# Graph-and-convolution layer: pieces for graph and gates, three streams stepped in turn, PSUM split by stage, vector work paced by size

## The chip, the core and the metric

The kernel runs on one core of a Trainium2 chip. The metric is the device time of one execution in microseconds (us); the time of a version is the median of its runs. The core's engines work side by side, each through its own list of instructions in order: PE multiplies matrices (PEld loads its weights), DVE does vector work, ACT evaluates functions, POOL does vector work too, SP issues the DMAs. PE writes its results to PSUM, which has eight banks of 128 x 512 float32; the other engines read them from there. Everything here is float32.

## The reference

For each of 32 batches x is 512 x 256 (nodes by features) and adj 512 x 512. Cut to what is computed:

```python
h = jnp.maximum(_layernorm(x, axis=-1), 0.0)
x = x + ref(h, adj, ...)

def ref(x, mask, ...):                                  # x is the normalised h
    xc = jnp.transpose(x, (0, 2, 1))
    h = jax.nn.relu(_bn(_conv1d(xc, conv1_w, 0), ...))   # 1 tap
    h = _bn(_conv1d(h, conv2_w, 8), ...)                 # 17 taps
    x_conv = jnp.transpose(jax.nn.relu(h + xc), (0, 2, 1))
    s = x @ w_se.T + b_se                                # 3 columns
    sq = jnp.sum(s * s, axis=-1)
    dist = sq[:, :, None] + sq[:, None, :] - 2.0 * jnp.einsum('bnd,bmd->bnm', s, s)
    A = jnp.exp(-dist) * mask
    msg = jax.nn.relu(x @ w_msg.T + b_msg)
    x_nmp = jnp.einsum('bnm,bmd->bnd', A, msg)
    x_in = jnp.concatenate([x_conv, x_nmp], axis=-1)
    gi, gh = x_in @ w_ih.T + b_ih, x @ w_hh.T + b_hh     # three gates each
    r, z = sigmoid(gi_r + gh_r), sigmoid(gi_z + gh_z)
    nn_ = jnp.tanh(gi_n + r * gh_n)
    return (1.0 - z) * nn_ + z * x
```

## The kernel before

The batches go in 8 groups of 4. Three stages work on three successive groups at once.

**Stage one** takes the batches of group g+1 one by one. `norm` gives DVE statistics (L189, L190), a POOL power (L146) and a scaling (L197) of the loaded `x_sb`; `norm_t` transposes it (PE L216, ACT L217) to `hT`, which also goes to DRAM as `hd`. `begin` ends with the load of batch b+2 (L97) and puts its `norm` on a list. `graph` then makes four `messages` (PE product to a PSUM bank, DVE bias L489/L490, ACT relu L493), the five small DVE steps of `factors` (L497 to L503), their transposes (L508, L512), `kernel_exp` (four small products L522, four ACT exponentials L526), four `masked` steps (PE transposes an `m_sb` block of adj, L533; DVE multiplies, L535) and two `gather` products, whose result goes to DRAM as `nd`. `rows` does the one-tap convolution into `h1` (ACT L226).

**Convolution.** The 17 taps are done for a group as 25 products with fewer multiplications. The operand of each is made by DVE from `h1`: five long ones `x1` (1,415 columns) and 25 short ones (471 columns), L237 and L240. At most four wait ahead (`AHEAD`), and the last rows of the next group may overwrite `h1` only once the 21st operand is made (`freed`, "rows wanted"). A product is two halves of four matmuls into `ps_c`; its weights `w` are read again from DRAM for each product (L339, two ahead). `summed` reads the products (ACT L368, L382; DVE L377, L379, L385, L386) and puts the additions that follow (DVE L355, L362, ACT L358) and, at the end of the group, eight evacuations (ACT L409, into `xconv`) on the list `SUMS`.

**Stage three** (`gates`) takes the batches of group g-1. `xconv` gets `hT` added (DVE L628) and a relu (ACT L629). For each half o of the features, four gate sums follow: hidden part of n, then r, z and the given part of n, each as one uninterrupted `matmul_sum` of 2 to 6 matmuls of 512 columns. Then DVE (L653, L667), ACT (L651, L661, L668) and three POOL steps (L674 to L676) make `o_sb`. `finish` transposes it back (PE L550), adds the residual (DVE L554) and stores it. It is called by `finish_waiting`, in the middle of the next `graph` after `kernel_exp`, or else after the first product of the next `gates`.

What sets the order on each engine is the order in which this program is written out; no scheduler moves anything (`manual_schedule`). `others` strings stage one and stage three together: the whole graph of one batch, then the whole gates of another. The loop at the end steps either `others` or one half of a convolution product, by a balance of their lengths; a "gap" in the graph calls for one half product. `pace` is called with the length of each PE step and puts vector work in between: it takes in turn from `SUMS`, the operands, the norms and, at first, the preparation of the convolution's weights, while its credit is positive. It has

```python
credit = min(credit + pe * 0.8, 4.0)
...
credit -= 0.9          # for each piece of work, whatever its length
```

Before the first group `first` does stage one of group 0 without a convolution, and what is left of the preparation is done behind it in one row. After the last group the gates of its four batches run alone, each step taking one piece from `SUMS`. Of the eight PSUM banks `ps_c` has two, `ps_acc` four (messages, rows, kernel, gather and gates share them) and `ps_tr` two (all transposes).

## Time and profile before

| | us |
|---|---|
| median of 3 runs | 2787.89 (2783.47 to 2789.23) |
| profiled execution | 2796.92 |
| its span, first to last instruction | 2795.1 |
| PE busy in it | 2402.3 (86%) |
| DVE busy | 1163.0 (42%) |
| ACT busy | 639.8 (23%) |
| POOL busy | 301.5 (11%) |
| first convolution product | 172.3 |
| mean granted TensorE clock | 0.923 of full speed |

The profiled execution is 9.0 us above the median. A row of waits says which engine at which line waited for what, and the total; a row of the timeline begins with the time from the start of the span and the length. "<-" names what ended an idle time. PE's busy time contains whatever a reduced clock adds to its instructions, so a busy PE is not PE at full speed.

### The profile page before, as it was taken

What the parts mean: (1) busy time and instruction counts of PE and PEld (TensorE: products, weight loads), DVE (VectorE), ACT (ScalarE), POOL (GpSimd) and SP (SyncE); (2) the same over time, 40 slices, a digit from 0 to 9 for tenths busy, and PEclk for the clock granted to TensorE, in tenths of its full rate; (3) what the DMA queues carried; (4) which work ended last, traced back from release to release, by engine and by line L of the source; (5) the groups of instructions that cost most, each with busy time, mean ns of one, the idle gap of its engine ahead of it and who ended that gap; (6) DMA issues with size and microseconds to landing.
All of it is one profiled execution on the core that took longest, in us unless ns stands there. A gap on an engine that the chain in (4) does not pass through costs nothing. (4 is left out here: it accounts for less than half of the span.)

```text
span 2795.1 us, 21712 instructions
## 1 busy us (share of the span) xinstructions
PE 2402.3 (86%) x8224; PEld 1516.8 (54%) x8224; DVE 1163.0 (42%) x1989; ACT 639.8 (23%) x930; POOL 301.5 (11%) x239
## 2 busy tenths in 40 slices
PE   5757878898889888889988889888899899999888
PEld 3446655555555555555555655555555555565543
DVE  5565543434544234353343532435333443454311
ACT  3321222122322123212132122321123122211211
POOL 1000001100111100111010111010111010112122
PEclk8879988999999999999999999999999999999999
DMA  5443332322322323322223322223222232223210
GB/s 195 145 180 128 114 129 84 113 83 94 105 94 89 107 72 106 109 90 87 83 98 106 103 90 87 91 98 113 80 98 81 89 112 87 83 91 102 72 61 27
DMA packets 132280, 277.88 MB, mean 99 GB/s; under 512 B 11984, under 2 KB 61520, under 8 KB 131536
## 3 DMA queue, kind: packets, MB, share of 16 engines
q1 hardware_dynamic: 132176, 276.50, 29.6%
q8 instruction: 65, 1.06, 0.2%
q14 instruction: 39, 0.32, 0.0%
HBM read 213.01 MB, written 63.44 MB: 99 GB/s over the span
## 5 line engine op out<-in xcount | busy, mean ns | idle before, releaser
L90 PE MATMUL ps_c<-x,w 128*128 128x228 f32 x3200 | 753.4, 387 | 125.1 <-issue 60.3
L90 PEld LDWEIGHTS ps_c<-x,w 128*128 128x128 f32 x3200 | 657.7, 209 | 237.3 <-issue 142.4
L90 PE MATMUL ps_acc<-xconv,wih 128*128 128x512 f32 x768 | 364.7, 597 | 13.1 <-ACT xconv L629 13.1
L90 PE MATMUL ps_acc<-hTb,whh 128*128 128x512 f32 x768 | 360.9, 602 | 5.3 <-DMA hTb<-hd 5.3
L90 PE MATMUL ps_acc<-xnb,wih 128*128 128x512 f32 x768 | 361.6, 593 | 0.0
L653 DVE SCALAR_TENSOR_TENSOR r<-ps_acc,vec,r 128x512 f32<-128x512 f32 x64 | 48.0, 751 | 615.4 <-ACT r L651 615.4
L674 POOL TENSOR_TENSOR gate_t<-hTb,r 128x512 f32<-128x512 f32 x64 | 88.2, 1378 | 1969.0 <-issue 1393.9
L90 PEld LDWEIGHTS ps_acc<-xnb,wih 128*128 128x128 f32 x768 | 146.1, 190 | 186.0 <-issue 186.0
L90 PEld LDWEIGHTS ps_acc<-xconv,wih 128*128 128x128 f32 x768 | 146.8, 191 | 178.4 <-issue 163.3
L90 PE MATMUL ps_acc<-at,msg 128*128 128x512 f32 x512 | 238.2, 620 | 5.0 <-DVE at L535 3.0
L90 PEld LDWEIGHTS ps_acc<-hTb,whh 128*128 128x128 f32 x768 | 147.9, 194 | 152.9 <-issue 146.2
L667 DVE TENSOR_TENSOR r<-ps_acc,r 128x512 f32<-128x512 f32 x64 | 44.2, 691 | 382.1 <-PE ps_acc L90 381.8
L533 PE MATMUL ps_tr<-ident,m_sb 128*128 128x128 f32 x512 | 92.9, 330 | 123.2 <-DVE at L535 62.1
L90 PEld LDWEIGHTS ps_acc<-at,msg 128*128 128x128 f32 x512 | 104.9, 206 | 122.2 <-issue 116.9
L240 DVE SCALAR_TENSOR_TENSOR x<-x,x 128x471 f32<-128x471 f32 (+1 forms) x184 | 160.2, 870 | 4.3
L237 DVE TENSOR_TENSOR x<-x 128x471 f32<-128x471 f32 x200 | 157.3, 803 | 1.4
L533 PEld LDWEIGHTS ps_tr<-ident,m_sb 128*128 128x128 f32 x512 | 71.0, 168 | 143.2 <-DVE at L535 90.3
L543 ACT ACTIVATE xnmp<-ps_acc 128x512 f32<-128x512 f32 x64 | 38.2, 597 | 464.3 <-PE ps_acc L90 464.3
L90 PE MATMUL ps_acc<-wmsg,hT 128*128 128x259 f32 x512 | 128.3, 394 | 10.4 <-ACT hT L217 10.4
L237 DVE TENSOR_TENSOR x<-h 128x1415 f32<-128x1415 f32 x40 | 83.2, 2098 | 94.0 <-ACT h L226 94.0
L661 ACT ACTIVATE z<-ps_acc,brz 128x512 f32<-128x512 f32 x64 | 44.0, 687 | 331.1 <-PE ps_acc L90 331.1
L90 PE MATMUL ps_acc<-hT,w 128*128 128x512 f32 x256 | 118.8, 612 | 0.1
(94 smaller groups left out, 1944.0 us busy)
## 6 DMA issues: line engine op xcount, KB each, us to landing
w<-wd SPq DMA_DIRECT2D x200, 512.0 KB, 3.6
m_sb<-in_adj_dram SPq DMA_DIRECT2D x128, 256.0 KB, 3.0
x_sb<-in_x_dram SPq DMA_DIRECT2D x32, 512.0 KB, 4.9
hd<-hT SPq DMA_DIRECT2D x32, 512.0 KB, 3.0
nd<-xnmp SPq DMA_DIRECT2D x64, 256.0 KB, 2.0
hTb<-hd SPq DMA_DIRECT2D x32, 512.0 KB, 4.4
xnb<-nd SPq DMA_DIRECT2D x64, 256.0 KB, 3.8
y<-in_x_dram SPq DMA_DIRECT2D x64, 256.0 KB, 4.1
```

What stands on the lines that cost most here:

```text
L90: nc.tensor.matmul(ps, lhsT, rhs, start=(i == 0), stop=(i == len(pairs) - 1))
L237: nc.vector.tensor_tensor(dst, get(a), get(b), op=ALU.subtract)
L240: nc.vector.scalar_tensor_tensor(dst, a, -2.0, b, op0=ALU.mult, op1=ALU.add)
L533: nc.tensor.transpose(ps[:, c, :], m[:, c * P : (c + 1) * P], ident)
L543: nc.scalar.activation(xnmp, ps, AF.Copy)
L653: nc.vector.scalar_tensor_tensor(r, ps_h, vec[:, _COL["b_hh"] + 2 * ND + o : _COL["b_hh"] + 2 * ND + o + 1], r, op0=ALU.add, op1=ALU.mult,)
L661: nc.scalar.activation(z, ps_z, AF.Sigmoid, bias=brz[:, ND + o : ND + o + 1])
L667: nc.vector.tensor_tensor(r, ps_n, r, op=ALU.add)
L674: nc.gpsimd.tensor_tensor(t, hT[:, o, :], r, op=ALU.subtract)
```

## The change

The arithmetic and the number of instructions on each engine stay as they are, except that two additions in the preparation of the weights become one that multiplies and adds. The pieces, their order and the buffers change:

- PSUM: `ps_acc` has two banks, for the gates alone. Two new banks `ps_g` take messages, rows, gather and two of the four products of `kernel_exp`; the other two of these go to `ps_tr`.
- `gather` is in two pieces, `factors` is called before the step of the fourth message ends, and the graph has no gaps.
- `gates` is written in pieces of two matmuls, split by source (hidden, xconv, xnb), in the order r, hidden n, z, given n. The addition and relu of `xconv` come after the first hidden product, and `finish_waiting` right behind them; the graph no longer calls it. POOL works in place in `o_sb`. Both `xnb` are loaded at the end of the gates before (two buffers instead of three), behind the loads of the residual on SP.
- The rows of all four batches come at the end of stage one.
- Stage one, stage three and the convolution are three streams; the loop steps the one with the least progress.
- `pace` takes a rate and charges each piece by its columns; the credit is capped at 1. ACT's copies and evacuations cost nothing but the constant. It is used behind the last group too, and the preparation is interleaved with stage one of group 0.

```diff
-    acc = ctx.enter_context(tc.tile_pool(name="acc", bufs=4, space=PSUM))
+    acc = ctx.enter_context(tc.tile_pool(name="acc", bufs=2, space=PSUM))
+    gps = ctx.enter_context(tc.tile_pool(name="gps", bufs=2, space=PSUM))
...
-            HT[b] = front.tile([P, ND, N], F32, name="hT", bufs=3)
+            HT[b] = front.tile([P, ND, N], F32, name="hT", bufs=4)
...
-        pss = [acc.tile([P, N], F32, name="ps_acc") for c in range(NT)]
+        pss = [pool.tile([P, N], F32, name=name) for pool, name in 2 * [(gps, "ps_g"), (tr, "ps_tr")]]
...
         for c in range(NT):
             messages(b, msg, c)
+            if c == NT - 1:
+                factors()
             yield 0.93
-        factors()
-        yield gap()
-        yield gap()
         factors_t()
         yield 0.67
-        yield gap()
         kernel_exp(at)
         yield 1.2
-        yield from finish_waiting()
-        yield gap()
         for n in range(NT):
             masked(b, at, n)
             yield 0.55
-        yield gap()
         for d in range(ND):
-            gather(b, msg, at, d)
-            yield 3.46
-        yield from between
+            yield from gather(b, msg, at, d)
...
+        def products(ps, o, g, first, last):
+            parts = [(whh, 0, hT[:, 0, :], hT[:, 1, :])]
+            parts += [(wih, 0, *x_in[:2]), (wih, ND, *x_in[2:])] if x_in else [None, None]
+            for k in range(first, last):
...
+                yield 1.73
         for o in range(ND):
+            yield from products(ps_r, o, 0, 0, 1)
             if o == 0:
+                while b not in evacuated:
+                    SUMS.pop(0)[0]()
+                xconv = XC.pop(b)[:, :, :N]
+                nc.vector.tensor_tensor(xconv, xconv, hT, op=ALU.add)
+                nc.scalar.activation(xconv, xconv, AF.Relu)
                 yield from finish_waiting()
+            yield from products(ps_r, o, 0, 1, 3)
...
+            yield from products(ps_h, o, 2, 0, 1)
...
+            yield from products(ps_z, o, 1, 0, 3)
...
+            yield from products(ps_n, o, 2, 1, 3)
...
-    def pace(pe):
-        credit = min(credit + pe * 0.8, 4.0)
+    def pace(pe, rate):
+        credit = min(credit + pe * rate, 1.0)
...
-            credit -= 0.9
+            credit -= 0.06 + 0.0011 * size
...
+    def stage_one(g):
+        new = range(g * G, (g + 1) * G)
+        for b in new:
+            yield from begin(b)
+            yield from graph(b)
+        yield "rows wanted"
+        for b in new:
+            yield from rows(b)
...
+            streams["one"] = [stage_one(g + 1), 77.0 * 0.86, 0.0]
+            streams["three"] = [stage_three(g - 1), 130.0, 6.0]
+        streams["conv"] = [conv, 82.5 * 0.96, 0.0]
+        rate = 0.4 if g > 0 else 0.7
...
+        while streams:
+            step(min(streams, key=lambda k: streams[k][2] / streams[k][1]))
+    for got in stage_three(NG - 1):
+        pace(got, 1.0)
```

Three places show what this does to the order. The first is PE's list around the masks of one batch in the middle of a group. The names are those of the stages above: `ps_c` is half a convolution product, `hTb,whh`, `xconv,wih` and `xnb,wih` are the three sources of the gates. Before:

```order
L522 MATMUL ps_acc<-right,left 128x512 x4
L550 MATMUL ps_tr<-ident,o_sb 128x128 x8
L90 MATMUL ps_c<-x_2359,w 128x228 x4
L533 MATMUL ps_tr<-ident,m_sb 128x128 x16
L90 MATMUL ps_c<-x_2359,w 128x228 x4
L90 MATMUL ps_acc<-at,msg 128x512 x8
L90 MATMUL ps_acc<-hTb,whh 128x512 x4
```

And now, from the third product of `kernel_exp` on:

```order
L525 MATMUL ps_g<-right,left 128x512
L525 MATMUL ps_tr<-right,left 128x512
L92 MATMUL ps_c<-x_2627,w 128x228 x4
L635 MATMUL ps_acc<-xnb,wih 128x512 x2
L536 MATMUL ps_tr<-ident,m_sb 128x128 x4
L635 MATMUL ps_acc<-hTb,whh 128x512 x2
L92 MATMUL ps_c<-x_2625,w 128x228 x4
L536 MATMUL ps_tr<-ident,m_sb 128x128 x8
L635 MATMUL ps_acc<-hTb,whh 128x512 x2
L536 MATMUL ps_tr<-ident,m_sb 128x128 x4
L92 MATMUL ps_c<-x_2625,w 128x228 x4
```

The sixteen mask transposes of a batch, which stood in a row, are now in groups of four and eight with gate products and half products between, and the finish (L550) is no longer there.

The second is the end of a group's stage one on PE (`ps_acc<-hT` and `ps_g<-hT` are the one-tap convolution). Before:

```order
L533 MATMUL ps_tr<-ident,m_sb 128x128 x16
L90 MATMUL ps_c<-x_2966,w 128x228 x4
L90 MATMUL ps_acc<-at,msg 128x512 x8
L90 MATMUL ps_acc<-hT,w_81 128x512 x12
L90 MATMUL ps_acc<-hTb,whh 128x512 x4
L90 MATMUL ps_acc<-xconv,wih 128x512 x2
L90 MATMUL ps_acc<-xnb,wih 128x512 x2
```

And now, where `x_3163` is the last product of a group and `x_3439` the first of the next:

```order
L635 MATMUL ps_acc<-xnb,wih 128x512 x2
L92 MATMUL ps_c<-x_3163,w 128x228 x4
L92 MATMUL ps_g<-hT,w_84 128x512 x10
L217 MATMUL ps_tr<-ident,x_sb 128x128 x4
L92 MATMUL ps_c<-x_3439,w 128x228 x4
L217 MATMUL ps_tr<-ident,x_sb 128x128 x4
L92 MATMUL ps_g<-wmsg,hT 128x259 x2
L92 MATMUL ps_c<-x_3439,w 128x228 x4
L92 MATMUL ps_g<-wmsg,hT 128x259 x2
L92 MATMUL ps_c<-x_3474,w 128x228 x4
```

The rows stand at the very end of the group, and the first product of the next, which needs operands made from them, follows them by four transposes. On ACT the evacuations of the group (L409, now L412) are then met like this, before:

```order
L409 ACTIVATE xconv<-y,bn_shift,bn_scale 128x3x3x57 x4
L526 ACT_TABLE_LOAD
L526 ACTIVATE at<-ps_acc 128x512 x4
L543 ACTIVATE xnmp<-ps_acc 128x512 x2
L629 ACTIVATE xconv<-xconv 128x2x512
L651 ACT_TABLE_LOAD
```

and now, from the last two exponentials of the first batch on:

```order
L529 ACTIVATE at<-ps_g 128x512
L529 ACTIVATE at<-ps_tr 128x512
L412 ACTIVATE xconv<-y,bn_shift,bn_scale 128x3x3x57 x5
L655 ACT_TABLE_LOAD
L655 ACTIVATE r<-ps_acc,brz 128x512
L668 ACTIVATE z<-ps_acc,brz 128x512
```

The relu of `xconv` (L629, now L650) stands seven rows ahead of these, behind two evacuations only, and five of the eight stand in a row ahead of the first sigmoid (L655).

The third is DVE's list where the statistics of a later batch (L189, now L190) meet the message evacuations (L489, now L492). Before:

```order
L489 TENSOR_TENSOR msg<-ps_acc,bmsg 128x256
L490 TENSOR_TENSOR aug<-ps_acc,bmsg 128x3
L189 BN_STATS st<-x_sb 128x6
L190 BN_AGGR mv<-st 128x2
L189 BN_STATS st<-x_sb 128x6
L190 BN_AGGR mv<-st 128x2
L189 BN_STATS st<-x_sb 128x6
L190 BN_AGGR mv<-st 128x2
L189 BN_STATS st<-x_sb 128x6
L190 BN_AGGR mv<-st 128x2
L145 TENSOR_SCALAR veps<-mv 128x4
L489 TENSOR_TENSOR msg<-ps_acc,bmsg 128x256
```

And now:

```order
L492 TENSOR_TENSOR msg<-ps_g,bmsg 128x256
L493 TENSOR_TENSOR aug<-ps_g,bmsg 128x3
L190 BN_STATS st<-x_sb 128x6
L191 BN_AGGR mv<-st 128x2
L190 BN_STATS st<-x_sb 128x6
L191 BN_AGGR mv<-st 128x2
L492 TENSOR_TENSOR msg<-ps_g,bmsg 128x256
L493 TENSOR_TENSOR aug<-ps_g,bmsg 128x3
L241 SCALAR_TENSOR_TENSOR x_5151<-x_4804,x_5151 128x1415
L380 TENSOR_TENSOR z<-ps_c,n 128x456
L674 TENSOR_TENSOR r<-ps_acc,r 128x512
L492 TENSOR_TENSOR msg<-ps_g,bmsg 128x256
```

All four pairs of statistics stood behind the first message; now two pairs stand between the second and the third, the other two come after the fourth, and a 1,415-column operand (L241) stands ahead of the gate's addition (L674).

## Rows read from the trace of the kernel before

**Rows 1.** Page, part 1: busy time, share of the span, instructions.

```profile
PE 2402.3 (86%) x8224; PEld 1516.8 (54%) x8224; DVE 1163.0 (42%) x1989; ACT 639.8 (23%) x930; POOL 301.5 (11%) x239
```

**Rows 2.** Timeline at a stretch without idle: start, length, engine, line, operation, count.

```profile
1705.66 1.70 PE L90 MATMUL ps_c<-x,w 128*128 128x228 f32 x8
...
1707.20 1.88 PE L90 MATMUL ps_acc<-hTb,whh 128*128 128x512 f32 x4
...
1708.92 1.88 PE L90 MATMUL ps_acc<-xconv,wih 128*128 128x512 f32 x4
```

**Rows 3.** Windows: length; PE, PEld, DVE, ACT, POOL busy; clock, DMA share, GB/s.

```profile
141.00:172.30 31.30, 5.11 (x15) 2.21 (x13) 23.38 (x27) 14.50 (x26) 0.00 (x0) 0.66 0.65 250
172.30:375.20 202.90, 169.18 (x708) 129.58 (x708) 102.82 (x200) 39.35 (x68) 4.03 (x4) 0.91 0.39 131
375.20:723.20 348.00, 303.76 (x1020) 192.44 (x1021) 138.59 (x244) 77.11 (x110) 35.56 (x26) 0.91 0.28 93
723.20:2082.10 1358.90, 1191.98 (x4114) 758.38 (x4113) 552.76 (x961) 316.18 (x448) 145.04 (x113) 0.93 0.29 95
2082.10:2404.00 321.90, 292.27 (x1030) 184.76 (x1029) 132.85 (x217) 79.14 (x112) 35.47 (x28) 0.96 0.29 94
```

**Rows 4.** PE's waits: line, waited for; total, times, longest.

```profile
PE ps_tr L533 <- DVE at L535: 62.1, 28, 5.7
...
PE ps_tr L508 <- DVE augl L503: 50.1, 17, 5.5
PE ps_c L90 <- ACT n L368: 38.7, 8, 6.6
...
PE ps_c L90 <- DMA w<-wd: 26.2, 1, 26.2
```

**Rows 5.** Timeline behind the load of a batch; idle time before and its releaser in brackets.

```profile
1488.28 0.43 DVE L189 BATCH_NORM_STATS2 st<-x_sb 128x6 f32<-128x256 f32 x1 [5.32 <-DMA x_sb<-in_x_dram]
...
1493.14 0.41 DVE L489 TENSOR_TENSOR msg<-ps_acc,bmsg 128x256 f32<-128x256 f32 x1
...
1494.71 3.41 PE L90 MATMUL ps_c<-x,w 128*128 128x228 f32 x8 [6.58 <-ACT n L368]
```

**Rows 6.** Timeline at the start of a group.

```profile
1744.71 5.52 DVE L355 TENSOR_TENSOR y<-y,z 128x1368 f32<-128x1368 f32 x3
...
1755.70 0.45 PE L508 MATMUL ps_tr<-ident,augl 128*128 128x128 f32 x1 [4.01 <-DVE augl L503]
...
1756.79 2.66 PE L90 MATMUL ps_c<-x,w 128*128 128x228 f32 x8
```

**Rows 7.** Groups by line and form: count, busy, mean ns of one, idle before.

```profile
L237 DVE TENSOR_TENSOR x<-x 128x471 f32<-128x471 f32 x200 | 157.3, 803 | 1.4
...
L355 DVE TENSOR_TENSOR y<-y,z 128x1368 f32<-128x1368 f32 x64 | 104.7, 1666 | 1.1
...
L237 DVE TENSOR_TENSOR x<-h 128x1415 f32<-128x1415 f32 x40 | 83.2, 2098 | 94.0 <-ACT h L226 94.0
L409 ACT ACTIVATE xconv<-y,bn_shift,bn_scale 128x513 f32<-128x513 f32 x64 | 76.4, 1290 | 54.5 <-DVE y L355 54.5
...
L226 ACT ACTIVATE h<-ps_acc,bn_shift,bn_scale 128x512 f32<-128x512 f32 x64 | 49.6, 777 | 87.0 <-PE ps_acc L90 79.4 <-DVE x L240 7.5
...
L651 ACT ACTIVATE r<-ps_acc,brz 128x512 f32<-128x512 f32 x64 | 43.9, 686 | 281.2 <-PE ps_acc L90 280.9
L628 DVE TENSOR_TENSOR xconv<-xconv,hTb 128x1024 f32<-128x1024 f32 x32 | 42.2, 1318 | 12.4 <-DMA hTb<-hd 7.5 <-ACT xconv L409 4.8
...
L629 ACT ACTIVATE xconv<-xconv 128x1024 f32<-128x1024 f32 x32 | 33.7, 1052 | 25.9 <-DVE xconv L628 25.9
...
L651 ACT ACT_TABLE_LOAD x24 | 30.8, 1283 | 125.7 <-PE ps_acc L90 125.7
```

**Rows 8.** Chain that ended last, from its last product to the transposes.

```profile
2783.81 0.70 DVE r L667
...
2789.40 1.77 PE ps_tr L550 x7
```

More of the change, by code (lines that the diff above doesn't have):

```diff
@@ L1 @@
 from contextlib import ExitStack
+from itertools import islice
 import concourse.bass as bass
@@ L269, in operands @@
         h1f = h1.rearrange("p r t -> p (r t)")
-        for x1 in fives(
+        for x1, size in fives(
             lambda k: h1f[:, k : k + 3 * N1 - 2 : 3],
@@ L539, in gather @@
     def gather(b, msg, at, d):
-        ps = acc.tile([P, N], F32, name="ps_acc")
-        matmul_sum(ps, [(msg[:, c, d * P : (d + 1) * P], at[:, c, :]) for c in range(NT)])
+        ps = gps.tile([P, N], F32, name="ps_g")
+        for c in range(NT):
+            nc.tensor.matmul(
+                ps, msg[:, c, d * P : (d + 1) * P], at[:, c, :], start=(c == 0), stop=(c == NT - 1)
+            )
+            if c == 1:
+                yield 1.73
         xnmp = front.tile([P, N], F32, name="xnmp", bufs=1)
@@ L751 @@
             nc.sync.dma_start(wflat[:, c, k0:k1, :], conv2_w[:, c, k0:k1, :])
-    def ahead_of(b):
-        yield from begin(b)
-        yield from rows(b)
-    def first():
-        yield from begin(0)
-        yield from rows(0)
-        for b in range(G):
-            yield from graph(b, ahead_of(b + 1) if b + 1 < G else ())
-    for got in first():
-        if got != "gap":
-            pace(got)
+    for got in stage_one_first():
+        pace(got, 1.2)
     while prepare_next():
@@ L782, in step_other, with step @@
+        streams["conv"] = [conv, 82.5 * 0.96, 0.0]
+        rate = 0.4 if g > 0 else 0.7
+        def step(name):
+            stream = streams[name]
+            got = next(stream[0], None)
             if got is None:
-                end = True
-                return False
-            if got == "rows wanted":
+                del streams[name]
+            elif got == "rows wanted":
                 while freed < g:
-                    step_conv()
-            elif got == "gap":
-                if not ended:
-                    step_conv()
-            else:
-                ahead += got * share
-                pace(got)
@@ L814 @@
-    for b in range((NG - 1) * G, B):
-        for _ in gates(b):
-            if SUMS:
-                SUMS.pop(0)()
+                    step("conv")
+            elif isinstance(got, tuple):
+                kind, value = got
+                if kind == "pe":
+                    stream[2] += value
+                    pace(value, rate)
+                elif kind == "rows":
+                    step("one")
+                elif kind == "group":
+                    del streams[name]
+            else:
+                stream[2] += got
+                pace(got, rate)
```

204 lines of the change are left out of this document (87 added, 117 removed).

## The prediction

> **What bounds the kernel now.** The busy times come first [rows 1]: PE 2402 of 2795 us, DVE under half, so PE sets the time and its 393 us of idle time are the first thing to win. Next comes what PE would need without idle time and at full speed. A stretch of the timeline in which nothing is waited for [rows 2] gives the pitch: the eight records of half a convolution product take 1707.20 - 1705.66 = 1.54 us, the four of a gate piece 1708.92 - 1707.20 = 1.72 us, 0.43 each. A steady group (groups 2 to 5) holds 50 half products, 77 us; four batches with 72 such records of 512 columns for gates, 16 for gathers and 8 for rows, 384 x 0.43 = 165 us; and messages, transposes and kernel products, which by their columns come to some 37 us. That is 279 us. The four steady groups, from one group's first product to the next's, lie in one window of 1358.9 us [rows 3], 339.7 each: 60.7 lost. PE is busy 1192.0 of it, so 41.7 us of a group are idle and 19.0 are reduced clock (0.93 granted), 0.45 us for each idle us. One sees where the clock falls: after a wait of 4.01 us the next half product takes at least 2.66 us instead of 1.54 [rows 6].
>
> The waits [rows 4] say who ends the idle time: DVE's mask multiplication 62 us, the kernel factors 50, ACT's reading of a convolution bank 39. Two stretches show why. In the first [rows 5] DVE's head instruction is the statistics of a batch whose load isn't there: 5.32 us idle, with the messages' evacuations behind it, the next at 1493.14; ACT waits for DVE, and PE waits 6.58 us for ACT. In the second [rows 6] three additions of 5.52 us in a row keep DVE from the messages, and the factors come 4.01 us late. DVE and ACT have the capacity; their work stands in the wrong order or in bursts.
>
> **The change part by part.** *Order in the middle of a group.* The statistics stand two pairs at a time, later, behind loads that had a batch's length to land; the additions are charged by size and mostly stand singly; half products and gate pieces lie between messages, factors, exponentials and masks. By the order and the pitches the cover from the exponentials' products to the first mask rises from 2.4 to 3.3 to 5 us, from the fourth mask to the gather it is 0 to 3.3 where it was 1.5; the reading of a convolution bank has 5 us and more where it had 0 to 5. I take the factor, mask, bank and load waits of a steady group as gone, except a gather that directly follows its last mask in two batches of four: DVE's multiplication and its start, 0.85 each, 1.7. Below nothing they can't cost; if half of them stay, 15 us come back (the rival of the smaller gain). Cutting products into pieces adds no instruction and I cost it at nothing: the pitch in rows 2 is the same across a change of the tile written, so no price is seen between pieces.
>
> *The end of a group.* This is new. Operands for the first product wait for the rows at the very end: ACT 0.78, the long operand 2.10, the short 0.80 [rows 7], less 0.4 of transposes: 3.3. The next operand: 2.1, of which DVE's part is two short steps and two message evacuations. Before the first gates' `xconv`: two additions of 1.67, two evacuations of 1.29, DVE 1.32, ACT 1.05, together 8.3, with a half product (1.54) and about 1 us of transposes beside it: 5.7. Then five evacuations stand ahead of the first sigmoid: 5 x 1.29 + table load 1.28 + 0.69 = 8.4, and z, which needs r's bank, has two gate pieces of 1.72 (less gaps already counted) to cover it: 5.2. Two further waits of an operand and a gather's bank: 1.9. Sum 18.2. At the least it is half (ACT starts earlier than I assume), at the most 26 (the same without any cover).
>
> *Finish.* From the last gate product to the transposes the chain takes 2789.40 - 2783.81 = 5.6 us [rows 8], through DVE, ACT and POOL. Finish stood behind the next kernel's exponentials with about 14 us of PE work ahead; now it follows the next gates' first piece, with 5.0 to 5.4, once 19. The addition waits in DVE's queue too, in one batch behind a long operand and a product's reading. I take 5.2, 4.0, 1.2 and 0: 10.4, and 0.5 for `xconv`. What is queued behind the transposes on PE is everything, half products included. The floor is 0.6 (5.6 less 5.0, DVE free) in three batches, 1.8; the ceiling 5.6 in all four, 22. The loads of the residual and of both `xnb` move behind the gates on SP; `w` stands behind them in the queue, but it is asked for two products ahead, so I cost that at nothing; without this cover it is a load's latency once a batch.
>
> *PSUM.* The gates have two banks instead of four: z needs the bank that the sigmoid of r empties, n the one of DVE's step, each with one to three pieces and usually a half product between, 2 to 5 us against 0.7 to 0.8 for the reader. I take 0; if readers are late it is the slower rival.
>
> The Trainium skill ("TensorE: Matmul & The Clock Gate", section "A second HAM failure mode: psum-queue depth-cycling") speaks against this part: it tells of a kernel that cycled through PSUM banks and whose TensorE idled briefly between matmul groups so often that the clock oscillated, although each matmul ran at its full rate. In the trace of before the gates cycle through four banks at full pitch [rows 2], so it shows no such loss; with two banks nothing here has shown it yet, and by this rule the slower rival would hold.
>
> *Sum for a steady group.* Idle 1.7 + 18.2 + 10.4 + 0.5 = 30.8 us, with 0.45 for the clock 44.7, against 60.7: 16.0 gained, times four 64. Group 1 (from 375.2) has much the same work and loses some 70 of its 348.0 [rows 3], as the first gates begin there; I keep a few us of the surplus: 20. Before the first product DVE works off the preparation, 23.4 us busy in 31.3 in which PE has 5.1 [rows 3], and PE's wait for `w` ends at 26.2 [rows 4]. Interleaved, this can fold into stage one; but there DVE also feeds PE, so of 4 to 30 I take 15. Group 0 has no gates; its 33.7 us of idle time [rows 3] should come near the steady 30.8, and the same clock: 5. Group 6 is idle 29.6 now [rows 3]: 0, with bounds of 5 either way. In the last group and its gates the chain of finish is as long as now: 0. Together 64 + 20 + 15 + 5 = 104 us. The profiled execution took 2796.9, so 2692.9; it lies 9 us above the median of 2787.9, to which the same share leads: 2787.9 x 2692.9 / 2796.9 = 2684 us.
>
> **The rivals.** *More is won.* ACT begins the evacuations when the sums are there and 7 of the 18.2 us disappear; with the clock 10 in each of six groups, 60 in all: 2624. For it: ACT is busy a quarter of the time. Against it: the order puts five evacuations in a row.
>
> *Much of it comes back elsewhere.* The vector queue, now in finer pieces but with little ahead, makes finish and masks wait: 6 us more idle in each of six groups, 8.7 with the clock, 52 in all: 2736. For it: operands lead the first products by 0 to 11 us of PE work where they led by 32 to 41, and long operands stand ahead of gate additions. Against it: DVE is free half the time.
>
> *The change doesn't do what it says.* The pieces are spread but each waits for the same chain as now: idle stays 42 in each group, and the 15 of the preparation are lost again where DVE feeds PE: 2788.
>
> *Two banks bind.* Every one of the 8 bank changes of a batch, 32 in a group, makes PE wait until a late sigmoid or DVE step has read its bank. At 0.45 us each that is 14.4 us, 20.9 with the clock, in seven groups 146: 2684 + 146 = 2830, slower than before. It decides from 104 / (7 x 1.45 x 32) = 0.32 us each. For it: DVE pieces of 1.7 and 2.1 us [rows 7] stand between gate steps and ACT has a row of evacuations. Against it: the cover above.
>
> **How the numbers follow.** My forecast (2650 to 2710) gets 0.45; more 0.13; the smaller gain (2710 to 2775) 0.22; no change 0.05; two banks 0.15. Forecast, more and smaller gain make 0.80, and reach from 2620 to 2775: that is the range. A difference of 0.2%, 5.6 us, is about what a measurement of this kernel can tell from none. Faster by more than that: 0.45 + 0.13 + 0.22 = 0.80; within it 0.05; slower 0.15.
>
> **What would show it.** Right: the waits for the factors, for ACT at the convolution's bank and for DVE at the masks fall from 151 us to under 50; new ones of 3 to 6 us appear at each group's first product, at the first `xconv` piece and at z; finish's transposes wait for POOL three times in four batches; a steady group takes near 324 us with the clock above 0.94; the first product comes near 157. Wrong: the waits of gate pieces for ACT or DVE at their banks are spread over all batches, or steady groups stay above 335 with the clock below 0.93.

## The result, and the profile after

The changed kernel takes 2697.26 us (median of 4 runs, 2696.22 to 2697.75) against 2785.68 us for the one before in the same comparison: 0.968 of it, 95% interval 0.967 to 0.970. That is 88 us less; forecast were 104, and the forecast time of 2684 us lies 13 us below the measured one. The first line of the page, to be held against [rows 1]:

```profile
PE 2389.5 (89%) x8224; PEld 1493.0 (55%) x8224; DVE 1187.6 (44%) x1989; ACT 637.8 (24%) x930; POOL 337.4 (13%) x239
```

The windows of the changed kernel, cut like [rows 3]: group 0, group 1, the four steady groups, group 6, and the last group with its gates (length; busy time of PE, PEld, DVE, ACT, POOL; granted clock, DMA share, GB/s).

```profile
171.90:366.50 194.60, 167.70 (x709) 127.71 (x709) 106.25 (x204) 39.47 (x68) 4.86 (x4) 0.92 0.40 137
366.50:695.30 328.80, 294.48 (x1021) 182.63 (x1021) 142.67 (x237) 77.16 (x111) 42.49 (x28) 0.94 0.29 99
695.30:1980.40 1285.10, 1176.89 (x4112) 740.48 (x4113) 572.53 (x960) 315.26 (x448) 170.25 (x112) 0.95 0.30 100
1980.40:2304.10 323.70, 295.10 (x1024) 184.80 (x1025) 136.57 (x215) 78.22 (x111) 40.36 (x26) 0.95 0.27 94
2304.10:2695.40 391.30, 348.66 (x1048) 201.44 (x1048) 130.56 (x150) 67.08 (x84) 69.21 (x48) 0.94 0.21 71
```

| stretch | before, us | after, us | gain | forecast |
|---|---|---|---|---|
| to the first convolution product | 172.3 | 171.9 | 0.4 | 15 |
| group 0 | 202.9 | 194.6 | 8.3 | 5 |
| group 1 | 348.0 | 328.8 | 19.2 | 20 |
| groups 2 to 5 | 1358.9 | 1285.1 | 73.8 | 64 |
| group 6 | 321.9 | 323.7 | -1.8 | 0 |
| group 7 and the last gates | 391.1 | 391.3 | -0.2 | 0 |
| span | 2795.1 | 2695.4 | 99.7 | 104 |

A steady group is 321.3 us. PE is idle for (1285.1 - 1176.9) / 4 = 27.1 us of it where it was 41.7; of the 294.2 busy us some 279 are work at full speed by the prediction's count, an estimate, which leaves 15 for the reduced clock, 19 before. Of the 73.8 us gained in the four groups 58.7 are idle time and 15.1 shorter busy time. PE's waits of 2 us and more in these four groups together, for comparison with [rows 4], which is of the whole span (line, waited for; total, times, longest):

```profile
PE ps_tr L559 <- POOL o_sb L683: 33.7, 12, 4.2
PE ps_c L92 <- issue: 21.6, 8, 3.4
PE ps_acc L635 <- ACT xconv L650: 20.7, 4, 5.2
PE ps_acc L635 <- ACT r L655: 16.5, 4, 4.1
PE ps_g L545 <- DVE at L538: 8.4, 8, 1.3
PE ps_tr L559 <- ACT at L529: 5.0, 4, 1.2
PE ps_tr L515 <- DVE y L563: 2.3, 4, 0.6
```

No mask, no factor that DVE is late with, no convolution bank and no load is among them any more (at L515 the factors' transposes wait for a bank of finish). One wait that [rows 4] does not show was the largest of the kernel before in its four steady groups:

```profile
PE ps_c L90 <- issue: 45.7, 8, 6.6
```

Eight half products wait there for a convolution bank, and the reading of that bank stands in DVE's queue behind the statistics of a late load, as in [rows 5]. With the 22.3 us for ACT at the same place this was 68 of the 167 idle us of the four groups. It is gone too: what is marked "issue" now are the first two operands of a group. Over the whole span the masks wait 10 us for DVE instead of 62, the factors 27 instead of 50, ahead of and in group 0. With ACT at the convolution's bank, which is gone, the three waits that the prediction named fall from 151 us to 36. What stands there now is finish (L559; 83 us in the whole span) and the start of a group (L650, L655 and the first operands, which show as "issue"). The second, in the timeline of one group:

```profile
1335.72 2.04 DVE L238 TENSOR_TENSOR x<-h 128x1415 f32<-128x1415 f32 x1 [3.37 <-ACT h L227]
...
1338.68 3.38 PE L92 MATMUL ps_c<-x,w 128*128 128x228 f32 x8 [3.37 <-issue]
...
1349.15 1.78 PE L92 MATMUL ps_c<-x,w 128*128 128x228 f32 x8 [2.02 <-issue]
...
1361.99 3.44 PE L635 MATMUL ps_acc<-xconv,wih 128*128 128x512 f32 x4 [5.18 <-ACT xconv L650]
...
1370.71 5.56 ACT L412 ACTIVATE xconv<-y,bn_shift,bn_scale 128x513 f32<-128x513 f32 x5
...
1377.58 0.69 ACT L655 ACTIVATE r<-ps_acc,brz 128x512 f32<-128x512 f32 x1
...
1378.32 2.68 PE L635 MATMUL ps_acc<-hTb,whh 128*128 128x512 f32 x3 [4.12 <-ACT r L655]
```

These are the four waits that the order of the change showed: the long operand behind the last row, the second operand, the xconv chain, and z behind five evacuations (L412) in a row. They measure 3.37, 2.02, 5.18 and 4.12 us; forecast were 3.3, 2.1, 5.7 and 5.2.

### The profile page after: what moved, and what is told of

Read it like the earlier page. It is cut to its first block, busy times and chain, and to the rows that moved or that the text cites. A ratio compares the mean times of both kernels' runs of the same rounds, so it can differ in the third digit from the quotient of the medians.

```text
span 2695.4 us, 21705 instructions
## 1 busy us (share of the span) xinstructions
PE 2389.5 (89%) x8224; PEld 1493.0 (55%) x8224; DVE 1187.6 (44%) x1989; ACT 637.8 (24%) x930; POOL 337.4 (13%) x239
## 3 DMA queue, kind: packets, MB, share of 16 engines
q8 instruction: 65, 1.06, 0.2%
## 4 chain that ended last, share of the span: by engine, by line
PE 78%; DVE 6%; ACT 4%; POOL 3%; issue 2%; DMA 1%; POOLq 0%; SPq 0%; DVEq 0%; ACTq 0%
PE ps_acc L635 36%; PE ps_c L92 21%; PE ps_g L545 8%; PE ps_g L92 7%; ACT xconv L412 2%; PE ps_tr L536 2%; POOL o_sb L681 1%; PE ps_tr L559 1%; PE ps_g L525 1%; PE ps_tr L217 1%; POOL o_sb L682 1%; DVE at L538 1%; DVE xconv L649 1%; POOL o_sb L683 1%; DMA x_sb<-in_x_dram 1%
## 5 line engine op out<-in xcount | busy, mean ns | idle before, releaser
L92 PE MATMUL ps_c<-x,w 128*128 128x228 f32 x3200 | 720.1, 370 | 45.1 <-issue 39.1
L635 PE MATMUL ps_acc<-xconv,wih 128*128 128x512 f32 x768 | 390.5, 634 | 40.7 <-ACT xconv L650 40.7
L635 PE MATMUL ps_acc<-hTb,whh 128*128 128x512 f32 x768 | 367.6, 607 | 25.9 <-ACT r L655 25.9
L681 POOL TENSOR_TENSOR o_sb<-hTb,r 128x512 f32<-128x512 f32 x64 | 97.1, 1517 | 1575.8 <-ACT r L675 1575.8
L545 PE MATMUL ps_g<-at,msg 128*128 128x512 f32 x512 | 248.9, 614 | 21.4 <-DVE at L538 20.5
L674 DVE TENSOR_TENSOR r<-ps_acc,r 128x512 f32<-128x512 f32 x64 | 44.1, 689 | 314.9 <-PE ps_acc L635 314.9
L545 PEld LDWEIGHTS ps_g<-at,msg 128*128 128x128 f32 x512 | 98.3, 195 | 123.0 <-issue 95.0
L492 DVE TENSOR_TENSOR msg<-ps_g,bmsg 128x256 f32<-128x256 f32 x128 | 54.0, 423 | 249.2 <-PE ps_g L92 249.2
L538 DVE TENSOR_TENSOR at<-ps_tr,at 128x512 f32<-128x512 f32 x128 | 86.1, 687 | 170.6 <-PE ps_tr L536 170.5
L241 DVE SCALAR_TENSOR_TENSOR x<-x,x 128x471 f32<-128x471 f32 (+1 forms) x184 | 153.8, 836 | 2.3
L92 PE MATMUL ps_g<-wmsg,hT 128*128 128x259 f32 x512 | 139.8, 400 | 16.4 <-DVE aug L493 14.3
L551 ACT ACTIVATE xnmp<-ps_g 128x512 f32<-128x512 f32 x64 | 38.2, 597 | 454.1 <-PE ps_g L545 348.8
L559 PE MATMUL ps_tr<-ident,o_sb 128*128 128x128 f32 x256 | 53.9, 344 | 90.6 <-POOL o_sb L683 83.0
L147 POOL TENSOR_TENSOR rstd<-veps,mhalf 128x4 f32<-128x4 f32 x32 | 38.2, 1194 | 762.7 <-DVE veps L146 762.5
L92 PEld LDWEIGHTS ps_g<-wmsg,hT 128*128 128x128 f32 x512 | 99.1, 199 | 61.5 <-issue 44.4
```

The lines of the kernel that those rows point to most:

```text
L92: nc.tensor.matmul(ps, lhsT, rhs, start=(i == 0), stop=(i == len(pairs) - 1))
L241: nc.vector.scalar_tensor_tensor(dst, a, -2.0, b, op0=ALU.mult, op1=ALU.add)
L492: nc.vector.tensor_tensor(msg[:, c, :], ps[:, :D], bmsg[:, :D], op=ALU.add)
L538: nc.vector.tensor_tensor(part, ps, part, op=ALU.mult)
L545: nc.tensor.matmul(ps, msg[:, c, d * P : (d + 1) * P], at[:, c, :], start=(c == 0), stop=(c == NT - 1))
L559: nc.tensor.transpose(ps[:, j, d * P : (d + 1) * P], o_sb[:, d, (c + j) * P : (c + j + 1) * P], ident)
```

## Where the gain comes from: taking the parts out

My theory is that PE lost time because vector work stood in bursts ahead of short chains, and that two things together cure it: vector work charged by length, and pieces of other streams between the links of a chain. The rival is that one of them does it all. Three runs undo one part each, a fourth adds one part to the kernel before. Steady groups are read from windows cut in the same way, from first product to first product. The kernel before, run beside each set of runs, took 2785.7 to 2792.1 us, so a difference of some 6 us between kernels of different sets is not clear of noise.

**Pacing by count.** The changed kernel with the old credit:

```diff
-        credit = min(credit + pe * rate, 1.0)
+        credit = min(credit + pe * 0.8, 4.0)
...
-            credit -= 0.06 + 0.0011 * size
+            credit -= 0.9
```

> The changed kernel with the pacing of the kernel before: credit 0.8 per us of PE work with a cap of 4 and 0.9 for each piece of vector work whatever its length; everything else as changed. Theory A (half or more of the gain comes from the vector work being spread): the waits of the factor transposes for DVE and of the convolution's banks return, 10 to 20 us of idle time in a steady group, and the time is 2740 to 2800. Theory B (the gain comes from the order of PE's pieces, which is unchanged here): at most 2710, the factor waits at most 40 us in all.

2755.99 us, 59 above the changed kernel. The size is theory A's, the places are not: the factors wait 11 us, less than with the change. Instead the first operands of the groups, the gathers and the messages wait, in this run's list of waits:

```profile
PE ps_c L92 <- issue: 64.5, 7, 10.3
PE ps_g L545 <- DVE at L538: 49.1, 18, 5.9
PE ps_g L92 <- DVE aug L493: 35.2, 12, 10.4
```

With the change these are 39.1, 20.5 and 14.3. Group 0, which has no gates to put between, grows from 194.6 to 212.6 us.

**Pacing by size alone**, in the kernel before (rates 0.4, 0.7, 1.2; the edit is the part of the change on `pace` and the sizes that it reads).

> The kernel before with only the pacing of the changed kernel: rates 0.4, 0.7 and 1.2, credit capped at 1, each piece of vector work charged by its columns; order of PE's pieces, PSUM and gates as before. Undoing the pacing in the changed kernel cost 59 us, writing the gate sums whole 57 us, of 91 us gained. Theory A (the parts help each other: spread vector work is of use only where PE's pieces are spread too): alone it gives less than half of that, 2765 or more, and the mask waits for DVE stay. Theory B (the parts add up): it gives about 59 us alone, 2720 to 2740.

2744.79 us against 2792.06 beside it: 47 us, between the two expectations and nearer to B. Pacing is worth 47 us alone and 59 with the rest, and the rest without it 30 (2785.7 to 2756.0), 77 of the 88 together: these two mostly add up, and the idea that pacing needs the pieces is wrong. The edit changes three things at once, the rate, the cap and the charge by length; which of them counts no run separates. The mask waits for DVE go from 62 to 29 us, though two others, 37.7 and 23.4 us in the kernel before, grow there, in this kernel's waits:

```profile
PE ps_tr L533 <- DMA m_sb<-in_adj_dram: 64.9, 28, 4.7
PE ps_tr L533 <- DVE y L554: 50.9, 6, 10.4
```

Sixteen mask transposes in a row outrun their loads as soon as DVE no longer holds them up. These are two waits that the spread masks and the moved finish of the change take away: its masks wait under 1 us for each.

**Gate sums written whole.**

```diff
-                yield 1.73
+                if o == 0 and k == 0 and not x_in:
+                    yield 1.73
+                elif k == last - 1:
+                    yield 1.73 * (last - max(first, 1 if o == 0 and g == 0 else 0))
```

> The changed kernel with the sums of the gates written in one row each again (r after its first hidden piece 2 pieces, z 3, the given part of n 2), so that the streams are stepped at whole sums; all else as changed. Theory A (the pieces between messages, factors, exponentials and masks are what covers their chains): waits at masks, gathers and factors return, 8 to 15 us of idle time in a steady group, and the time is 2740 to 2790. Theory B (half products of the convolution are fine enough to cover them): the time is within 10 us of 2697.

2753.95 us, 57 above; a steady group is idle 35.6 us, 8.6 more, as theory A had it. The growth is at finish (102.5 us, from 83.0), the factors (36.8, from 26.5) and the gathers (28.2, from 20.5); the masks, which theory A named too, stay at 10. With whole sums the rest of the change, pacing included, gains 32 us, where pacing alone gave 47 in the kernel before: without the pieces the rest of the new order brings nothing.

**One pool of four banks.**

```diff
-    acc = ctx.enter_context(tc.tile_pool(name="acc", bufs=2, space=PSUM))
-    gps = ctx.enter_context(tc.tile_pool(name="gps", bufs=2, space=PSUM))
+    acc = ctx.enter_context(tc.tile_pool(name="acc", bufs=4, space=PSUM))
...
-        pss = [pool.tile([P, N], F32, name=name) for pool, name in 2 * [(gps, "ps_g"), (tr, "ps_tr")]]
+        pss = [acc.tile([P, N], F32, name="ps_acc") for c in range(NT)]
```

> The changed kernel with one pool of four PSUM banks for gates, messages, rows, kernel products and gathers, as the kernel before had, instead of two for the gates and two for the others; the four kernel products all use it. Theory A (two banks for the gates cost only where z waits behind the evacuations at a group's start): those waits of gates for ACT's sigmoid (25.9 us) go, the mask transposes get their banks free of kernel products, and the time is 2680 to 2700. Theory B (the split is part of the gain, since in one pool a gate waits for banks held by messages that DVE has not read): new waits of gates for DVE at messages, and 2715 or more.

2725.8 us (2718 to 2733), 28 above. What each theory said of the waits: z no longer waits for r's sigmoid (25.9 us before this edit, none now), as A has it, and no wait of gates for messages appears, against B; only the kernel products wait 16 us for ACT. But the time is B's. The four steady groups:

```profile
700.00:1998.40 1298.40, 1196.36 (x4113) 745.80 (x4113) 571.60 (x960) 316.91 (x448) 170.41 (x112) 0.95 0.30 99
```

PE is idle less (102.0 us for 108.2) and busy 19.5 us longer with the same instructions, at the same granted clock of 0.95. The longer time is at the four products of `kernel_exp`. In the changed kernel, with two banks of `ps_g` and two of `ps_tr`, all four run side by side, and the next work begins 1.07 us after the first:

```profile
1046.76 0.69 PE L525 MATMUL ps_g<-right,left 5*128 5x512 f32 x1
...
1047.83 1.81 PE L92 MATMUL ps_c<-x,w 128*128 128x228 f32 x8
```

In the same batch with one pool only three find a bank. The fourth waits until ACT has read one, and then runs alone:

```profile
1054.19 1.13 PE L524 MATMUL ps_acc<-right,left 5*128 5x512 f32 x6
1056.00 1.12 PE L524 MATMUL ps_acc<-right,left 5*128 5x512 f32 x2 [0.67 <-ACT at L528]
1057.05 1.86 PE L91 MATMUL ps_c<-x,w 128*128 128x228 f32 x7
```

That is 2.86 us for 1.07. The wait stands in each of the 16 batches of the steady groups, and 16 x 1.12 = 17.9 us are most of the 19.5. In the kernel before, with one pool too, the fourth product never waits: no gate sum was open at that point. So the split pays by a bank for each of the four products, and not for the reason of theory B; that it is an open gate sum that holds the fourth bank is inferred. The two runs lie 15 us apart, so the size of 28 us is rough.

## The waits that the change brought

The second question is whether finish and the group's start cost what the waits say: is an idle time of PE gained when what it waits for is moved?

**Finish behind r's first pieces.**

```diff
-                yield from finish_waiting()
             yield from products(ps_r, o, 0, 1, 3)
+            if o == 0:
+                yield from finish_waiting()
```

> The changed kernel with one edit: the transposes of the previous batch's finish come behind the xconv and xnb pieces of r instead of behind the first hidden piece, so that about 3.4 us more gate work, and what is stepped in between, covers the chain DVE, ACT, POOL. Theory A (the 83 us in which the finish transposes wait for POOL are a cost of this place alone): these waits fall under 20 us, nothing takes their place, and the time falls by 70 to 110 us (each idle us also costs about 0.45 us of reduced clock), to about 2610. Theory B (the wait only uncovers the next one, the xconv relu or the bank of z, which end late anyway): waits for ACT at the gates grow by as much as the finish waits fall, and the time stays within 15 us of 2697.

2691.58 us (runs at 2687.1 and 2696.0): 6 us, not clear of noise, and theory B. The waits of this run:

```profile
PE ps_acc L635 <- ACT xconv L650: 133.2, 30, 14.0
...
PE ps_tr L559 <- POOL o_sb L684: 5.4, 1, 5.4
```

Finish lost nearly all of its 83 us, and the relu of `xconv` took 92 more: without the transposes in front of it, the first xconv piece comes too early. The masks now wait 25.9 us for finish's addition too. The end, where no masks and no half products lie between, gained (373.0 us for 391.3); the four steady groups lost 11:

```profile
691.80:1988.00 1296.20, 1165.44 (x4113) 731.65 (x4113) 584.35 (x960) 315.00 (x448) 172.21 (x112) 0.95 0.30 99
```

**xconv ahead, alone and with finish later.** The addition and relu for the next batch are written before the last gate sum of the one before, if its convolution is evacuated:

```diff
+    def made_ready(b):
+        if b not in READY:
+            READY[b] = xconv = XC.pop(b)[:, :, :N]
+            nc.vector.tensor_tensor(xconv, xconv, HB[b], op=ALU.add)
+            nc.scalar.activation(xconv, xconv, AF.Relu)
+        return READY[b]
...
             if o == 0:
                 load_gates(b + 1)
+            elif b + 1 in evacuated:
+                made_ready(b + 1)
```

> The changed kernel with only the sum and relu of xconv written ahead, finish left where the change puts it. Moving finish alone gave 6 us, both together 102. Theory A (the two waits stand one behind the other on the same place of PE, and each hides the other: only taking both away shortens it): xconv ahead alone gives 5 to 25 us, 2672 to 2692, and the finish transposes still wait 75 to 95 us for POOL. Theory B (the xconv chain on DVE is what delays finish's adds and gate steps, so moving it is most of the gain): 2640 or less and finish waits under 50 us.

> The changed kernel with finish behind the first two sources of r, as in the run that only moved it, and in addition the sum and relu of xconv for the next batch written ahead of the last gate sum of the batch before, where its convolution is already evacuated. Theory A (moving finish only uncovered the relu of xconv, 133 us of waits, and this wait is one of place too): waits for POOL at finish and for ACT at xconv come to under 60 us together, steady groups go to 305 to 313 us, the part after the last group's first product to about 365, and the time to 2580 to 2630. Theory B (ACT and DVE are the limit at these places whatever the order): another wait for them takes over, steady groups stay at 318 or more and the time above 2670.

Alone it gives 2690.82 us, 6 us and again not clear of noise; together with the moved finish 2595.02, 102 us. Both theories A hold, but for the two waits of the second, which come to 66 us together where it had under 60. The waits of the first, and then of both together:

```profile
PE ps_tr L559 <- POOL o_sb L692: 76.1, 23, 5.4
...
PE ps_acc L644 <- ACT xconv L622: 39.1, 7, 7.4
```

```profile
PE ps_acc L644 <- ACT xconv L622: 59.8, 8, 14.0
...
PE ps_tr L559 <- POOL o_sb L693: 6.4, 4, 5.4
```

Two chains end at the same place of PE, POOL's for finish and DVE's and ACT's for xconv. Each covered the other; the list of waits shows only the one that is met first, with its full time. What is left at `xconv` is the first batch of each group, whose convolution is not evacuated in time. Steady groups are 310.3 us (expected 305 to 313), idle 22.8 each, and their granted clock is 0.97. Of the 44.1 us that the four groups gain, 17 are idle time and 27 shorter busy time, so the higher clock gives more than the waits themselves:

```profile
673.70:1914.70 1241.00, 1149.79 (x4113) 724.80 (x4113) 578.90 (x960) 315.47 (x448) 164.91 (x112) 0.97 0.31 104
```

**Gates that start later.** One number: the loop steps the stream whose progress is the smallest share of its length, and `"three"` starts with a progress of 20.0 instead of 6.0, so its first steps come later.

> The changed kernel with one number changed: stage three starts with a handicap of 20 instead of 6 in the balance of the streams, so that the first gates of a group come some 14 us of gate work later and the last ones end behind the convolution. Theory A (the waits of 5.2 us for xconv and 4.1 us for the bank of z at a group's start are there because the eight evacuations are asked for too early): both go, 9 us of idle time and 13 us in each group that has gates, and the time is 2600 to 2650; the first product of a group still waits its 3.4 us. Theory B (gates left alone at the end of a group lack half products between them and wait for their own DVE and ACT steps): new waits at the group's end eat it, and the time stays within 20 us of 2697.

2667.03 us, 30 gained, between the two. The waits for xconv and z at a group's start go (40.7 to 3.4 us, 25.9 to 3.6), but the factors wait 47 us for 27, and the first product now waits 8.4 us instead of 3.4, in the timeline of one group:

```profile
1315.59 6.53 ACT L412 ACTIVATE xconv<-y,bn_shift,bn_scale 128x513 f32<-128x513 f32 x6
...
1321.93 0.73 ACT L227 ACTIVATE h<-ps_g,bn_shift,bn_scale 128x512 f32<-128x512 f32 x1
1322.69 2.03 DVE L238 TENSOR_TENSOR x<-h 128x1415 f32<-128x1415 f32 x1 [15.28 <-ACT h L227]
...
1326.13 3.38 PE L92 MATMUL ps_c<-x,w 128*128 128x228 f32 x8 [8.39 <-issue]
```

The pacing charges an evacuation next to nothing, so six of them come out in a row, and the last row of `h1`, on which every operand of the next group depends, is behind them on ACT.

**Rows that end earlier.** The factor on the length of stage one goes from 0.86 to 1.00, that of the convolution from 0.96 to 1.06, so both are stepped sooner against the gates.

> The changed kernel with the weights of two streams changed (stage one from 0.86 to 1.00, the convolution from 0.96 to 1.06), so that a group's rows and last product come before its last gate pieces instead of behind them. Theory A (the waits at a group's first two products, 3.4 and 2.0 us, are the chain from the last row through ACT and DVE and vanish as soon as about 7 us of gates lie behind the rows): they fall under 1 us together, 5 us of idle time and some 7 us per group, and the time is 2640 to 2670; the xconv wait shrinks too, since the sums of the group are done before. Theory B (the sums and operands that must be made meanwhile wait for DVE in the same queue): at the first products 3 us or more remain, and the time is within 15 us of 2697.

2636.32 us, 61 gained, more than theory A's, and only half for its reason. The first product waits 1.1 us for 3.4, as expected; the second 3.2 to 5.7, where it was 2.0, so the waits marked "issue" stay at 40 us. What went are the xconv wait (12.5 us for 40.7) and the one at z. In the steady groups idle time falls by 14 us and busy time by 27, at a clock of 0.97. The second product's wait has the mechanism of [rows 5]: DVE's head is the statistics of a batch whose load isn't there, and the operand stands behind it:

```profile
1313.90 0.43 DVE L190 BATCH_NORM_STATS2 st<-x_sb 128x6 f32<-128x256 f32 x1 [3.85 <-DMA x_sb<-in_x_dram]
...
1316.86 0.64 DVE L241 SCALAR_TENSOR_TENSOR x<-x,x 128x471 f32<-128x471 f32 x1
1317.60 1.86 PE L92 MATMUL ps_c<-x,w 128*128 128x228 f32 x4 [5.66 <-issue]
```

**All together.** Finish later, xconv ahead and the two weights:

> The changed kernel with the edits of two runs together: finish later with xconv ahead (2595 us), and the weights that let a group's rows and last product come before its last gate pieces (2636 us). Theory A (they take away different waits: finish and xconv 10 us a group, evacuations and z some 9 us a group): steady groups come to 298 to 303 us and the time to 2525 to 2560. Theory B (both move the same wait, since gates that end later also find xconv ready): 2580 to 2600.

2566.77 us (ratio to the kernel before 0.919, 0.917 to 0.921), between the two expectations: of 102 and 61 us they keep 130. With the gates' start at 10.0 (the handicap) besides:

> The kernel with both moves (2567 us) and a handicap of 10 instead of 6 for stage three, so that the first gates of a group start behind the kernel products of its first batch. There each steady group still waits 4.2 us for xconv and 5.2 us for finish's addition. Theory A (both are the first gates meeting the sums, evacuations and operands of the new group on DVE and ACT): both go, steady groups come to 295 to 299 us, the time to 2500 to 2530. Theory B (the operands of the second product, 6.7 us now, are what DVE is late with, and the rest moves behind them): steady groups stay above 304 and the time within 10 us of 2567.

2532.07 us, 0.907 of the kernel before (0.904 to 0.909) and 165 us below the changed one. The time is 2 us above theory A's range. A steady group is 298.5 us, inside it, but one of the two waits did not go: xconv's is now a single one of 10 us a group, finish's addition went. The four steady groups:

```profile
675.70:1869.50 1193.80, 1129.52 (x4115) 711.07 (x4114) 577.94 (x961) 314.74 (x448) 169.24 (x112) 0.98 0.33 108
```

Idle time is 16.1 us a group, in few pieces, and of the 282.4 busy us only 3.4 are reduced clock, by the same estimate of 279.

**The preparation.** None of it between the steps of group 0's stage one; all behind:

```diff
-        return None if next(prepare, "done") == "done" else 700
+        return None if not flush or next(prepare, "done") == "done" else 700
...
+    flush = False
     for got in stage_one_first():
         pace(got, 1.2)
+    flush = True
```

> The changed kernel with none of the preparation of the convolution's weights put between the steps of group 0's stage one; all of it is done in a row behind it, as only its rest was in the kernel before. Theory A (interleaving is worth its 15 us and more, and something else in the new order of stage one costs them: the first product came at 171.9 us although I had forecast 157): without it the first product comes at 200 us or later, and the time is 2725 or more. Theory B (DVE's work is only moved, since each piece of preparation holds up the messages and masks behind it as long as it takes): the first product comes at 165 to 185 us and the time is 2690 to 2710.

2714.84 us, and the first product at 188.7, between the theories. PE is through with stage one by 139 us and then stands still:

```profile
139.00:188.70 49.70, 0.10 (x2) 0.05 (x1) 39.82 (x53) 28.97 (x52) 0.00 (x0) 0.55 0.73 291
```

So the interleaving is worth 17 us against none; the kernel before had put part of the preparation into stage one already, and 23.4 us of DVE were left. In the changed kernel nearly all of these 40 us stand within stage one, which ends late for it: its factors wait up to 8.2 us, while preparation steps stand ahead of the messages' additions (L492), the long ones (L296, L297) 1.75 us each:

```profile
102.42 1.75 DVE L296 TENSOR_TENSOR g<-wraw 128x1536 f32<-128x1536 f32 x1
104.21 1.76 DVE L297 TENSOR_TENSOR g<-g,wraw 128x1536 f32<-128x1536 f32 x1
105.88 0.68 DVE L290 SCALAR_TENSOR_TENSOR gg<-g 128x512 f32<-128x512 f32 x1
...
107.21 0.42 DVE L492 TENSOR_TENSOR msg<-ps_g,bmsg 128x256 f32<-128x256 f32 x1
...
108.55 0.47 PE L511 MATMUL ps_tr<-ident,augl 128*128 128x128 f32 x1 [8.20 <-DVE augl L506]
```

The pacing charges each step of the preparation 700 columns, whether it is 512 columns or two instructions of 1,536: here it does not go by length.

## Why the prediction was right, and where it was off

**What bounds the kernel**: right. The gain is idle time of PE in the steady groups and group 1, with the clock behind it (58.7 and 15.1 us in the steady groups), and the waits named are those that went. The list of waits left out the largest one of the steady groups, 45.7 us at half products; it has the mechanism of [rows 5], so the reading held for it too.

**Order in the middle of a group**: right. I took the factor, mask, bank and load waits of a steady group as gone but for 1.7 us at the gather; the gathers wait 8.4 us in four groups, 2.1 each. The load wait is not gone everywhere: the statistics still stand in front of a late load at a group's start, which shows once the rows end earlier.

**The end of a group**: 18.2 forecast, 3.37 + 2.02 + 5.18 + 4.12 = 14.7 measured. Each of the four was sized within 1.1 us; the fifth term of 1.9 did not come.

**Finish**: 10.4 forecast; 33.7 + 5.0 + 2.3 = 41.0 us in four groups, 10.3 in each. That it comes so near is in part luck. POOL's chain, which I had priced, is 33.7 of it, 8.4 in each group, three times in four batches as forecast; the other 7.3 are banks of `ps_tr`, held by a kernel product (5.0) or by finish's own addition (2.3), for which I had no term. And the reading was incomplete: I treated the wait as a cost of finish's place, and moving finish alone gave back some 6 of 83 us.

**PSUM**: the gates' two banks cost 26 us in all, at z behind the evacuations at a group's start and nowhere else; the cover I worked out holds. The Trainium skill's warning ("TensorE: Matmul & The Clock Gate", "A second HAM failure mode: psum-queue depth-cycling") did not come true here: with two banks the steady groups' clock rose from 0.93 to 0.95, and one pool of four gave the same 0.95. What I overlooked is the other side of the split: the four kernel products need four free banks, and with one pool, beside gates in pieces, they do not get them.

**Idle time and clock**: 30.8 idle and 13.9 reduced clock forecast, 27.1 and 15 measured; the two errors partly cancel. The factor of 0.45 us per idle us is no constant: it is 0.56 here, 0.38 with finish moved alone, 0.21 in the fastest run, all by the estimate of 279 us. The 2.66 us of [rows 6] are the length of a row and belong against the 1.70 of [rows 2], not against the pitch of 1.54.

**Before the first product**: the step that failed. I took 15 us of a range of 4 to 30 and got 0.4. I counted DVE's busy time as movable into its gaps; but PE of that stretch waits for DVE through short chains, and what is put in front of their links delays them. Stage one grew by as much as the remainder shrank: PE's last transposes of it end at 165.9 us instead of 146.1, and the wait for `w` falls from 26.2 to 6.0.

**Group 0 and 1, group 6, the end**: 8.3, 19.2, -1.8 and -0.2 us for 5, 20, 0 and 0.

**From the profile to the median**: the sum against the profiled execution was 104 for 99.7. The other 9 us lie in the step to the median: the profiled execution of before was 9 us above its median, that of the change is not, and I scaled both by the same share.

**The rivals**: the change did what it says, the gates' banks did not bind beyond z, and neither more nor much less came. The rival "more is won" asked for evacuations that begin earlier; that this is to be had was shown by the later runs, not by this kernel.

## What to carry to other kernels

Work on an engine's queue should be charged by its length when it is put between other work: one number for all pieces lets the long ones bunch up. Here the charge, with a lower rate and a smaller cap, was worth 47 us; that the charge alone does it is not shown. A list of waits names the chain that is met first; before moving it, look for a second chain that ends at the same place, since both had to be moved here to gain either (some 6 us each, 102 together). When three streams are balanced, try to let the ones end first whose results open the next round (61 us here). Work that several banks let run side by side needs all of them free at once: one bank short cost 1.8 us a batch.

## What was unexpected of the hardware

DVE's instructions are held up while POOL works. In the middle of a finish of the changed kernel:

```profile
1434.81 1.26 POOL L682 TENSOR_TENSOR o_sb<-z,o_sb 128x512 f32<-128x512 f32 x1
1435.00 1.14 DVE L502 COPY augr<-aug 128x80 f32<-128x80 f32 x1
...
1436.15 1.26 POOL L683 TENSOR_TENSOR o_sb<-r,o_sb 128x512 f32<-128x512 f32 x1
1436.20 2.30 DVE L649 TENSOR_TENSOR xconv<-xconv,hTb 128x1024 f32<-128x1024 f32 x1
```

The same copy takes 0.21 us and the same addition 1.23 us in the group's first batch, where POOL is idle. Here the copy ends as POOL's step does, and the addition 1.1 us after the next one. The copy's mean goes from 0.21 us in the kernel before to 0.41, POOL's busy time from 301.5 to 337.4 us with as many instructions: the change put POOL's three steps beside the factors. That they now work in place in `o_sb` does not explain it: the shortest of each takes 1.26 us in both kernels. The Trainium skill ("SBUF — State Buffer", "Who interferes with whom") says that the two engines share a port pair: a copy of DVE in a two-port mode or POOL, whichever issues first, holds it for the whole instruction while the other waits, and an addition of DVE with two inputs in SBUF contends with POOL's reads. These lines agree: each of the two DVE instructions takes longer by nearly what was left of POOL's step.

Second, the reduced clock depends on more than the sum of idle time. A steady group of the changed kernel, with 27.1 us idle in eleven pieces, has 294.2 busy us; with finish moved alone it is idle longer, 32.7 us, and yet busy only 291.4, with the same instructions. In the fastest run 16.1 us, of which 10 are one piece, go with 282.4. What in the pattern of the waits decides it, these runs do not separate.
